# A recurrent layer in four streams: 256 places for sums and powers, two tiles of squares, and another order of the step

## The chip, the core and the metric

The kernel runs on one core of a Trainium2 chip. A core has five engines that run side by side and wait for one another through semaphores: TensorE (PE in the profile, with its weight loads shown as PEld), VectorE (DVE), ScalarE (ACT), GpSimd (POOL) and SyncE (SP), which here only starts transfers. Each engine takes its instructions strictly in the order of its own queue. The metric is the device time of the whole program in microseconds, and the figure for a kernel is the median of several runs.

## The reference, cut to what matters

The program computes four residual layers on an image of 256 x 256 places with 32 channels. The first is a gated projection behind two normalisations, the second and third are Sobel magnitudes of a pooled image behind a group norm, and the fourth, where most of the time goes, is a recurrent net of two cells over T = 256 steps and S = 256 sequences:

```python
for j in range(L):                       # L = 2 cells, hidden size H = 128
    zz = concatenate([z, h_all[j]]) @ W_cell[j] + b_cell[j]      # S x 4H
    zz = _group_norm(zz, gn_gamma[j], gn_beta[j])                # four groups of H
    i, f, o, g = split(zz, 4)
    c = sigmoid(f) * c_all[j] + sigmoid(i) * tanh(g)
    h = sigmoid(o) * tanh(c)
    z = z + h
x_hat = x_t + z @ W_out + b_out
```

So a step needs the h and the c of the step before it in each cell, and the second cell needs the h of the first.

## The kernel before, in words

The front part (loading and transposing the image, the projection layer, the two Sobel layers) takes the first 629 us of the profile. Its constants stand in one tile `kt` of 13 matrices of 128 x 128, loaded in one transfer from ACT's queue (line 99); together with the weights `wv4` and `wg4` and the small matrices `avg` and `spread` they stay in the pool `const`, which lives to the end of the program. The image `xb` is in the pool `big2`, which is closed before the recurrence (`second.close()`, line 547), so that its memory is used again.

The recurrence (function `recurrence`, from line 811) splits the work into four streams: cell l = 0 or 1, and half h = 0 or 1 of the sequences (128 each, one for each partition). I write a stream as two digits, cell and half, after the name of an operation: `sq01` is the operation `sq` of cell 0, half 1. For each stream and step there are these operations (function `one`, lines 887 to 976):

- `x` (one call, `project`, lines 866 to 885, for all four streams): bias (line 876) and input (line 879) are multiplied into a fresh PSUM bank `zz`, 128 x 512, for each stream. PE.
- `m` (line 911): the stream's own previous h times its weights is added; `i` (line 906): for cell 1, the h of cell 0 too. PE.
- `sq` (line 919): squares of `zz` are written to the stream's tile `sq`. ACT. The tiles are made once (line 760), one for each stream, with an extra column that holds epsilon for each group.
- `rd` (line 924): sums over each group give four numbers a sequence, `ve`. DVE. They go to place t % 32 of the tile `sums` (SLOTS = 32).
- `pw` (line 927): these numbers to the power -1/2, `rs`, to place t % 32 of the tile `roots`. POOL, its only work here.
- `si`, `sf`, `so`, `tg` (line 900): the gates, each 128 x 128, with `rs` as the scale. ACT. Three of them share a tile `ga`, and `so` has a tile `go`.
- `ig` (947), `fc` (951), `c` (955): the new cell state. DVE.
- `th` (line 966): tanh of the state. ACT.
- For half 0 of each cell the gate `so` and the state `c` are turned on PE first (`to`, line 959, and `T`, line 963), `th` reads the turned state, and `h` (line 969, DVE) writes the turned hidden state `hT`. For half 1, `h` is made straight (line 973, DVE), turned by `T` (line 963) and copied by `e` (line 975, DVE).
- `hs` (line 986, DVE) adds the two cells' h for the output. Every eight steps one output is made: `o0` and `o1` (lines 998 and 1008, PE), `of` (1017, ACT), `ot` (1023, DVE) and eight transfers from SP's queue.

`ga`, `go`, `fc`, `th`, `zn` and `h` come from a pool `unit` of four buffers for each name, so one for each stream. The order of everything is written out by hand: the table `PLAN` gives each operation of each stream a planned time within its step, `OUT` those of the common ones, a step is PERIOD = 7.6 later than the step before, and all of it is sorted by planned time (line 1047) and issued in that order. The planned times set the order in each engine's queue and nothing else. The two cells are therefore worked on some steps apart: in one period of 7.6 the queue holds stream 00 of step t, 01 of step t - 1 or t, and 10 and 11 of steps t - 1 to t - 3.

The code of the waits is not in the kernel text: the layer that builds the program puts a wait into each instruction that reads what another engine writes, or writes where another engine or an earlier instruction has been. An instruction carries one wait; where it needs a second one, a separate semaphore instruction stands in front of it in the same queue.

Of the kernel before, what the change touches and what calls it, by code (L numbers as in the profile page):

```python
# [11 lines left out]
F32 = mybir.dt.float32  # L12
BF16 = mybir.dt.bfloat16
AF = mybir.ActivationFunctionType
ALU = mybir.AluOpType
AX = mybir.AxisListType
PSUM = bass.MemoryType.PSUM

S = 256
T = 256  # L20
C = 32
J = 4
NB = T // J
P = 128
H = 128
L = 2
# [4 lines left out]
CELL_EPS = 1e-5  # L31


K_GN, K_CEN, K_AVG, K_SOBEL = 0, 1, 2, 3
NK = 3 + 10


# [23 lines left out]
def net_kernel(  # L61
# [33 lines left out]

    ident = cp.tile([P, P], F32, name="ident")
    make_identity(nc, ident)
    kt = cp.tile([P, NK, P], F32, name="kt")
    nc.scalar.dma_start(out=kt, in_=consts)

    def eps_tile(value, name):
        t = cp.tile([P, 1], F32, name=name)
# [17 lines left out]
    bout4 = per_channel(b_out, "bout4")  # L120

    def four_times(w, n, name):
        t = cp.tile([P, n], F32, name=name)
        for j in range(J):
            nc.gpsimd.dma_start(out=t[j * C : (j + 1) * C, :], in_=w)
        return t
# [14 lines left out]
    def busy(psum, n, rhs=None):  # L141

        junk = psum.tile([P, S], F32, name="junk", tag="junk", bufs=1)
        for _ in range(n):
            nc.tensor.matmul(
                junk, lhsT=ident, rhs=kt[:, 0:2, :] if rhs is None else rhs, start=True, stop=True
            )

    def new_stats():
# [2 lines left out]
    def group_norm(stats, psum, before, after, rhs=None):  # L152

        mv = small.tile([P, nc.vector.BN_AGGR_DIM], F32, name="mv")
        nc.vector.bn_aggr(mv, stats)
        busy(psum, before, rhs)
        pm = psum.tile([P, 1], F32, name="pm", tag="pm", bufs=1)
        nc.tensor.matmul(pm, lhsT=kt[:, K_GN, :], rhs=mv[:, 0:1], start=True, stop=True)
        busy(psum, 2, rhs)
        mean = small.tile([P, 1], F32, name="mean")  # L160
        nc.vector.tensor_copy(mean, pm)
        d = small.tile([P, 1], F32, name="d")
        nc.vector.tensor_sub(d, mv[:, 0:1], mean)
        q = small.tile([P, 1], F32, name="q")
        nc.vector.scalar_tensor_tensor(q, d, d, mv[:, 1:2], ALU.mult, ALU.add)
        pv = psum.tile([P, 1], F32, name="pv", tag="pm", bufs=1)
        nc.tensor.matmul(pv, lhsT=kt[:, K_GN, :], rhs=q, start=True, stop=True)
        busy(psum, after, rhs)
        std = small.tile([P, 1], F32, name="std")
        nc.scalar.activation(std, pv, AF.Sqrt, bias=gn_eps)  # L170
        scale = small.tile([P, 1], F32, name="scale")
        nc.vector.reciprocal(scale, std)
        bias = small.tile([P, 1], F32, name="bias")
        nc.vector.scalar_tensor_tensor(bias, mean, -1.0, scale, ALU.mult, ALU.mult)
        return scale, bias
# [1 line left out]
    KS = NST // 4  # L177


    avg = cp.tile([P, KS, KS, J], F32, name="avg")  # L180
    nc.gpsimd.memset(avg, 0.0)
    for ks in range(KS):
        nc.gpsimd.tensor_copy(avg[:, ks, ks, :], kt[:, K_AVG, 0:P:C])
    spread = cp.tile([P, KS * J, C], F32, name="spread")
    for g in range(4):
        rows = slice(g * C, (g + 1) * C)
        nc.gpsimd.tensor_copy(
# [46 lines left out]
    with tc.tile_pool(name="ln", bufs=4) as lnp:  # L234
        rstd = lnp.tile([P, 2 * S], F32, name="rstd", bufs=1)
        with tc.tile_pool(name="ps_ln", bufs=6, space=PSUM) as ps_ln, tc.tile_pool(
            name="ps_var", bufs=1, space=PSUM
        ) as ps_var:
            cen = lnp.tile([P, P], F32, name="cen", bufs=1)
            nc.vector.tensor_scalar(cen, kt[:, K_CEN, :], gn[0], None, ALU.mult)  # L240
            pcb = ps_var.tile([P, 1], F32, name="pcb")
            nc.tensor.matmul(pcb, lhsT=kt[:, K_CEN, :], rhs=gn[1], start=True, stop=True)
            cb = lnp.tile([P, 1], F32, name="cb", bufs=1)
            nc.vector.tensor_copy(cb, pcb)
            pvar = ps_var.tile([P, 2 * S], F32, name="pvar")
            sqs = {}

            def variance(k, g, ks):
                nc.tensor.matmul(
                    pvar[g * C : (g + 1) * C, :],  # L250
                    lhsT=avg[:, ks].rearrange("p k j -> p (k j)"),
                    rhs=sqs.pop(k),
                    start=ks == 0,
                    stop=ks == KS - 1,
                )

            for i, (k, g, ks) in enumerate(pairs):
                pc = ps_ln.tile([P, 2 * S], F32, name="pc")
                nc.tensor.matmul(pc, lhsT=cen, rhs=pair(xa, k), start=True, stop=True)  # L259
                sqs[k] = lnp.tile([P, 2 * S], F32, name="sq", bufs=10)  # L260
                nc.scalar.activation(sqs[k], pc, AF.Square, bias=cb)
                nc.vector.tensor_scalar(pair(xb, k), pc, cb, None, ALU.add)
                if g == 3 and ks:
                    for q in pairs[i - 7 : i - 3]:
                        variance(*q)
            for q in pairs[-4:]:
                variance(*q)
            std = lnp.tile([P, 2 * S], F32, name="std", bufs=1)
            nc.scalar.activation(std, pvar, AF.Sqrt, bias=ln_eps)
            table(AF.Sigmoid, std[:, 0:1])  # L270
            nc.vector.reciprocal(rstd, std)
            for _ in range(9):
                nc.tensor.matmul(
                    pvar[:, 0:S], lhsT=ident, rhs=kt[:, 0:2, :], start=True, stop=True
                )
        with tc.tile_pool(name="ps_sp", bufs=8, space=PSUM) as ps_sp:
            for i, (k, g, ks) in enumerate(pairs):
# [18 lines left out]
            junk = ps_sp.tile([P, 2 * S], F32, name="pb")  # L296
            for _ in range(4):
                nc.tensor.matmul(
                    junk[:, 0:S], lhsT=ident, rhs=kt[:, 0:2, :], start=True, stop=True
                )  # L300


# [441 lines left out]
class RecurrentInputs:  # L744
# [5 lines left out]
    def __init__(self, tc, ctx, xa):  # L750
        self.nc = nc = tc.nc
        self.xa = xa
        kp = ctx.enter_context(tc.tile_pool(name="keep", bufs=1, reuse_waits="tile"))
        self.mhalf = kp.tile([P, 4], F32, name="mhalf")
        nc.gpsimd.memset(self.mhalf, -0.5)

        self.sqs = {}
        for l in range(L):
            for h in range(2):
                sq = self.sqs[l, h] = kp.tile([P, 4, H + 1], F32, name=f"sq{l}{h}")  # L760
                nc.gpsimd.memset(sq[:, :, H : H + 1], CELL_EPS)
        self.xts = []
        for i in range(self.NX):
            self.xts.append(kp.tile([P, self.XT, J, P], F32, name=f"xt{i}"))
        for k in range(self.NX):
            self.load(k)
# [11 lines left out]
    def of(self, t, rows):  # L778
# [5 lines left out]


SLOTS = 32
PERIOD = 7.600
BLOCKS = 2
PLAN = {
    (0, 0): dict(  # L790
        m=0.300, sq=1.814, rd=1.883, pw=2.686, tg=4.187, sf=4.207, so=4.930, fc=5.023,
        to=5.301, si=5.390, ig=5.646, c=5.897, T=6.647, th=7.011, h=7.161,
    ),
    (0, 1): dict(
        m=4.328, sq=5.425, rd=6.234, pw=8.247, sf=8.370, tg=8.501, si=8.549, fc=8.711,
        so=8.739, ig=9.246, c=9.459, th=9.581, h=10.106, T=10.657, e=11.627,
    ),
    (1, 0): dict(
        i=10.749, m=14.225, sq=14.912, rd=15.578, pw=16.964, si=17.174, so=17.198, tg=17.865,
        to=17.992, ig=18.493, sf=18.507, fc=18.957, c=19.359, T=19.440, th=19.713, h=20.542,  # L800
    ),
    (1, 1): dict(
        i=17.550, m=17.552, sq=18.681, rd=19.727, pw=20.540, si=20.935, sf=21.284, fc=21.803,
        tg=21.870, ig=21.907, c=22.633, so=23.115, th=23.210, h=23.269, T=23.489, e=24.537,
    ),
}
OUT = dict(x=7.804, hs=31.517, o0=35.554, o1=38.043, of=39.159, ot=39.669)

def recurrence(tc, out, ident, weights, inputs, general):
# [22 lines left out]
    up = ctx.enter_context(tc.tile_pool(name="unit", bufs=4))  # L834

    kp = ctx.enter_context(tc.tile_pool(name="norm", bufs=1))
    sums = kp.tile([P, 2 * L, SLOTS, 4], F32, name="ve")
    roots = kp.tile([P, 2 * L, SLOTS, 4], F32, name="rs")
    sp = ctx.enter_context(tc.tile_pool(name="state", bufs=2))
    hp = ctx.enter_context(tc.tile_pool(name="hid", bufs=6))  # L840
    op = ctx.enter_context(tc.tile_pool(name="outp", bufs=1))
# [45 lines left out]
    def one(name, l, h, t):  # L887
# [6 lines left out]
        def gate(g, func):  # L894

            x, scale = (get("zn"), 1.0) if general else (get("zz"), get("rs")[:, g : g + 1])
            if g == 2:
                v["go", l, h] = up.tile([P, H], F32, name="go")
            dst = get("go") if g == 2 else gates(get("ga"), min(g, 2))
            nc.scalar.activation(dst, gates(x, g), func, scale=scale)  # L900
            v["left", l, h, t] -= 1
# [15 lines left out]
                )  # L917
        elif name == "sq":
            nc.scalar.activation(  # L919
                sqs[l, h][:, :, 0:H], four(get("zz")), AF.Square, scale=float(H**-0.5)  # L920
            )
        elif name == "rd":
            ve = v["ve", l, h] = sums[:, 2 * l + h, t % SLOTS, :]
            nc.vector.tensor_reduce(ve, sqs[l, h], AX.X, ALU.add)  # L924
        elif name == "pw":
            rs = v["rs", l, h] = roots[:, 2 * l + h, t % SLOTS, :]
            nc.gpsimd.tensor_tensor(rs, get("ve"), inputs.mhalf, ALU.pow)  # L927
            v["ga", l, h] = up.tile([P, 3 * H], F32, name="ga")
            if not general:
# [32 lines left out]
                v["pt", l, h] = bank("pt", ("pt", l, h), [P, 2, 2 * H])  # L962
            nc.tensor.transpose(get("pt")[:, 1, 0:P], get("c" if turned else "h"), ident)  # L963
        elif name == "th":
            th = v["th", l, h] = up.tile([P, H], F32, name="th")
            nc.scalar.activation(th, get("pt")[:, 1, 0:P] if turned else get("c"), AF.Tanh)  # L966
        elif name == "h":
            if turned:
# [124 lines left out]
```

## Time and profile before

| | |
|---|---|
| median of 3 runs | 2632.31 us (2629.91 to 2633.71) |
| the profiled execution, its own time | 2632.46 us |
| its span, first to last instruction | 2630.6 us |
| start of the first `x` of the recurrence | 628.9 us |
| start of the last `x` | 2608.3 us |
| granted TensorE clock over the span | 0.991 |
| power on POOL, line 927 | 1024 of 1023 ns |
| sum on DVE, line 924 | 1024 of 689 ns |
| squares on ACT, line 919 | 1024 of 609 ns |

In the views a row of the timeline gives the start in us, the duration in us, engine, line, operation, tiles, shapes and count, and in brackets the idle time of the engine just before it with what ended it. Durations of matmuls are modelled and overlap with the next one, so the starts tell more than the ends.

### The profile page before, as it was taken

The numbers are of one execution on the slowest core, as the hardware profiler recorded it, in microseconds if no ns is written. First come the engines' busy times: TensorE is split into PE (matmuls) and PEld (weight loads), VectorE is DVE, ScalarE is ACT, GpSimd is POOL, SyncE is SP. The second block draws the span as 40 slices with busy tenths as digits, with TensorE's granted clock in tenths as the row PEclk, the third lists the DMA queues.
The fourth block names the chain that finished last, engine by engine and source line by source line (L and its number), as shares of the span: only waits on it lengthen the run. The fifth ranks groups of instructions, "written<-read, shape, count | busy, mean of one in ns | idle before, by whom it ended". The sixth has DMA issues, their size and how long they took to land.

```text
span 2630.6 us, 43062 instructions
## 1 busy us (share of the span) xinstructions
PE 2574.9 (98%) x11181; PEld 1007.4 (38%) x11181; DVE 2329.4 (89%) x6735; ACT 2296.4 (87%) x6948; POOL 1298.0 (49%) x1288
## 2 busy tenths in 40 slices
PE   7999999998999999999999999999999999999997
PEld 4533433433333333333333333333333333333332
DVE  6788799796999999999999999999999999999996
ACT  5677677675999999999999999999999999999996
POOL 2211276463555555555555555555555555555553
PEclk9899999999999999999999999999999999999998
DMA  4000000002010000001010101010000001000000
GB/s 146 1 1 1 18 1 1 0 1 49 1 25 8 18 12 14 16 10 20 6 21 5 21 5 21 5 24 9 18 12 14 16 10 20 6 5 5 5 5 10
DMA packets 110744, 38.68 MB, mean 15 GB/s; under 512 B 74852, under 2 KB 107653, under 8 KB 110488
## 3 DMA queue, kind: packets, MB, share of 16 engines
q1 hardware_dynamic: 108452, 34.54, 6.1%
q8 instruction: 92, 1.51, 0.3%
q14 instruction: 164, 1.34, 0.2%
q10 hardware_dynamic: 1236, 0.99, 0.1%
q0 software_dynamic: 800, 0.30, 0.1%
HBM read 10.63 MB, written 8.39 MB: 7 GB/s over the span
## 4 chain that ended last, share of the span: by engine, by line
PE 93%; DVE 3%; ACT 2%; POOL 1%; issue 1%; DMA 1%; DVEq 0%; SPq 0%; ACTq 0%; POOLq 0%
PE zz L911 35%; PE zz L906 16%; PE zz L879 8%; PE pt L963 6%; PE pv L315 5%; PE pg L489 4%; PE pg L449 3%; PE zz L876 3%; PE pg L339 2%; PE pt L959 2%; PE pg L315 1%; PE px L1008 1%; PE pc L259 1%; PE px L998 1%; PE pb L280 1%
## 5 line engine op out<-in xcount | busy, mean ns | idle before, releaser
L927 POOL TENSOR_TENSOR rs<-ve,mhalf 128x4 f32<-128x4 f32 x1024 | 1047.1, 1023 | 953.5 <-DVE ve L924 953.5
L911 PE MATMUL zz<-wc,hT 128*128 128x512 f32 x2040 | 1069.0, 612 | 1.4 <-DVE hT L969 1.2
L900 ACT ACTIVATE ga<-zz,rs 128x128 f32<-128x128 f32 x3072 | 974.7, 376 | 53.6 <-POOL rs L927 47.3
L924 DVE TENSOR_REDUCE ve<-sq 128x4 f32<-128x516 f32 x1024 | 705.2, 689 | 69.4 <-ACT sq L919 49.1
L919 ACT ACTIVATE sq<-zz 128x512 f32<-128x512 f32 x1024 | 623.7, 609 | 53.8 <-PE zz L911 14.2
L906 PE MATMUL zz<-wc,hT 128*128 128x512 f32 x1024 | 524.4, 594 | 0.0
L911 PEld LDWEIGHTS zz<-wc,hT 128*128 128x128 f32 x2040 | 306.7, 189 | 355.8 <-DVE hT L969 168.7
L900 ACT ACTIVATE go<-zz,rs 128x128 f32<-128x128 f32 x1024 | 394.1, 385 | 0.0
L947 DVE TENSOR_TENSOR c<-ga 128x128 f32<-128x128 f32 x1024 | 298.4, 291 | 65.1 <-ACT ga L900 58.6
L951 DVE TENSOR_TENSOR fc<-ga,c 128x128 f32<-128x128 f32 x1020 | 297.9, 292 | 5.5 <-ACT ga L900 4.1
L955 DVE TENSOR_TENSOR c<-c,fc 128x128 f32<-128x128 f32 x1020 | 286.7, 281 | 8.8
L879 PE MATMUL zz<-fx,xt 32*128 32x512 f32 x2048 | 265.8, 589 | 0.0
L333 DVE TENSOR_TENSOR o<-pv,sg 128x512 f32<-128x512 f32 x256 | 158.1, 681 | 43.3 <-PE pg L315 37.7
L959 PEld LDWEIGHTS pt<-ident,go 128*128 128x128 f32 x512 | 71.1, 139 | 290.8 <-ACT go L900 283.4
L906 PEld LDWEIGHTS zz<-wc,hT 128*128 128x128 f32 x1024 | 172.7, 209 | 9.4 <-issue 9.4
L963 PEld LDWEIGHTS pt<-ident,c 128*128 128x128 f32 x512 | 70.9, 139 | 268.9 <-DVE c L955 260.9
L966 ACT ACTIVATE th<-c 128x128 f32<-128x128 f32 x512 | 166.0, 324 | 4.6 <-DVE c L955 1.2
L963 PE MATMUL pt<-ident,h 128*128 128x128 f32 x512 | 157.9, 308 | 10.8 <-DVE h L973 8.5
L330 ACT ACTIVATE sg<-pg 128x512 f32<-128x512 f32 x256 | 138.6, 599 | 31.0 <-PE pg L315 26.3
L966 ACT ACTIVATE th<-pt 128x128 f32<-128x128 f32 x512 | 146.2, 286 | 18.9 <-PE pt L963 18.9
L969 DVE TENSOR_TENSOR hT<-pt,th 128x128 f32<-128x128 f32 x512 | 144.1, 282 | 13.8 <-ACT th L966 13.8
L315 PE MATMUL pv<-xb,wv 32*128 32x512 f32 x512 | 156.2, 619 | 0.0
(169 smaller groups left out, 2991.6 us busy)
## 6 DMA issues: line engine op xcount, KB each, us to landing
xt<-xa SPq DMA_DIRECT2D x256, 64.0 KB, 2.0
nat<-in_x_dram SPq DMA_DIRECT2D x16, 512.0 KB, 7.1
out_dram<-st SPq DMA_DIRECT2D x252, 32.0 KB, 1.7
wc<-in_L_conv_W_cell_dram SPq DMA_DIRECT2D x2, 512.0 KB, 4.8
kt<-in_consts_dram ACTq DMA_DIRECT2D x1, 832.0 KB, 6.1
wv<-in_L_conv_Wv_dram POOLq DMA_DIRECT2D x4, 32.0 KB, 4.2
wg<-in_L_conv_Wg_dram POOLq DMA_DIRECT2D x4, 32.0 KB, 6.2
out_dram<-st ACTq DMA_DIRECT2D x4, 32.0 KB, 3.3
```

What stands on the lines that cost most here:

```text
L315: nc.tensor.matmul(ps, lhsT=w[rows, half * P : (half + 1) * P], rhs=mn, start=True, stop=True)
L879: nc.tensor.matmul(v["zz", l, h, t], lhsT=inputs.of(t, r), rhs=fx[r, :], start=False, stop=l == 0 and t == 0,)
L900: nc.scalar.activation(dst, gates(x, g), func, scale=scale)
L906: nc.tensor.matmul(get("zz"), lhsT=v["hT", 0, t][:, seqs], rhs=wc[:, l, 0, :], start=False, stop=t == 0)
L911: nc.tensor.matmul(get("zz"), lhsT=v["hT", l, t - 1][:, seqs], rhs=wc[:, l, 1, :], start=False, stop=True,)
L919: nc.scalar.activation(sqs[l, h][:, :, 0:H], four(get("zz")), AF.Square, scale=float(H**-0.5))
L924: nc.vector.tensor_reduce(ve, sqs[l, h], AX.X, ALU.add)
L927: nc.gpsimd.tensor_tensor(rs, get("ve"), inputs.mhalf, ALU.pow)
L947: nc.vector.tensor_mul(c, gates(get("ga"), 0), gates(get("ga"), 2))
L951: nc.vector.tensor_mul(fc, gates(get("ga"), 1), get("c"))
L963: nc.tensor.transpose(get("pt")[:, 1, 0:P], get("c" if turned else "h"), ident)
L966: nc.scalar.activation(th, get("pt")[:, 1, 0:P] if turned else get("c"), AF.Tanh)
```

## The change

Five things are edited together:

- `sums` and `roots` get one place for each of the 256 steps, where there were 32 (for weights of the plain case, which these inputs are).
- Each stream gets two tiles of squares, used on even and odd steps.
- `go` and `th` get eight buffers where they had four.
- `PLAN` and `OUT` are other numbers. By engine, the order within a period changes in these places. ACT: `si01` and `sf01` change places among the four gates of stream 01, `tg10` and `si10` among those of stream 10, and the order `tg00 sf00 th10 so00 si00` becomes `sf00 so00 th10 si00 tg00`; `of` comes in front of stream 01's gates instead of behind them. DVE: `ig01` stands in front of `fc01`; `hs` moves from between these two to between `h10` and `ig00`, and comes 2.9 of planned time sooner after its step; `ot` moves from in front of `e11` to in front of `h11`. PE: `o0` moves from in front of `to00` to behind it. Everything else keeps its order on each engine, POOL too.
- The first two constant matrices get a tile of their own, `kg`, with a transfer of its own in front of that of the other eleven; these eleven, `wv4`, `wg4`, `avg` and `spread` move to the pool `big2`, whose memory is free again when the recurrence begins.

```diff
-K_GN, K_CEN, K_AVG, K_SOBEL = 0, 1, 2, 3
+K_GN, K_CEN = 0, 1
+K_AVG, K_SOBEL = 0, 1
...
-    kt = cp.tile([P, NK, P], F32, name="kt")
-    nc.scalar.dma_start(out=kt, in_=consts)
+    kg = cp.tile([P, 2, P], F32, name="kg")
+    nc.scalar.dma_start(out=kg, in_=consts[:, 0:2, :])
+    kt = big2.tile([P, NK - 2, P], F32, name="kt")
+    nc.scalar.dma_start(out=kt, in_=consts[:, 2:NK, :])
...
-        t = cp.tile([P, n], F32, name=name)
+        t = big2.tile([P, n], F32, name=name)
...
-    avg = cp.tile([P, KS, KS, J], F32, name="avg")
+    avg = big2.tile([P, KS, KS, J], F32, name="avg")
...
-    spread = cp.tile([P, KS * J, C], F32, name="spread")
+    spread = big2.tile([P, KS * J, C], F32, name="spread")
...
-                sq = self.sqs[l, h] = kp.tile([P, 4, H + 1], F32, name=f"sq{l}{h}")
-                nc.gpsimd.memset(sq[:, :, H : H + 1], CELL_EPS)
+                for i in range(2):
+                    sq = self.sqs[l, h, i] = kp.tile([P, 4, H + 1], F32, name=f"sq{l}{h}{i}")
+                    nc.gpsimd.memset(sq[:, :, H : H + 1], CELL_EPS)
...
     (0, 0): dict(
-        m=0.300, sq=1.814, rd=1.883, pw=2.686, tg=4.187, sf=4.207, so=4.930, fc=5.023,
-        to=5.301, si=5.390, ig=5.646, c=5.897, T=6.647, th=7.011, h=7.161,
+        m=0.300, sq=1.315, rd=2.221, pw=2.435, sf=3.687, so=3.851, si=5.257, tg=5.350,
+        fc=5.575, to=5.625, ig=5.913, c=6.078, T=7.351, th=7.469, h=7.525,
     ),
     (0, 1): dict(
-        m=4.328, sq=5.425, rd=6.234, pw=8.247, sf=8.370, tg=8.501, si=8.549, fc=8.711,
-        so=8.739, ig=9.246, c=9.459, th=9.581, h=10.106, T=10.657, e=11.627,
+        m=5.465, sq=5.522, rd=6.135, pw=6.225, si=8.272, tg=8.393, sf=8.539, so=8.617,
+        ig=9.064, fc=9.178, c=9.275, th=9.750, h=10.406, T=11.076, e=11.164,
     ),
     (1, 0): dict(
-        i=10.749, m=14.225, sq=14.912, rd=15.578, pw=16.964, si=17.174, so=17.198, tg=17.865,
-        to=17.992, ig=18.493, sf=18.507, fc=18.957, c=19.359, T=19.440, th=19.713, h=20.542,
+        i=11.801, m=14.599, sq=15.182, rd=15.403, pw=15.916, tg=17.278, so=17.665, si=17.826,
+        sf=17.853, ig=18.025, to=18.521, fc=18.583, c=18.914, T=19.851, th=20.220, h=20.862,
     ),
     (1, 1): dict(
-        i=17.550, m=17.552, sq=18.681, rd=19.727, pw=20.540, si=20.935, sf=21.284, fc=21.803,
-        tg=21.870, ig=21.907, c=22.633, so=23.115, th=23.210, h=23.269, T=23.489, e=24.537,
+        i=17.726, m=17.895, sq=18.421, rd=19.343, pw=19.789, si=21.949, sf=21.973, fc=22.060,
+        tg=22.379, ig=22.470, c=22.779, so=22.984, th=23.047, h=23.842, T=24.141, e=24.465,
     ),
-OUT = dict(x=7.804, hs=31.517, o0=35.554, o1=38.043, of=39.159, ot=39.669)
+OUT = dict(x=7.840, hs=28.575, o0=29.152, o1=30.235, of=30.667, ot=30.900)
...
-    sums = kp.tile([P, 2 * L, SLOTS, 4], F32, name="ve")
-    roots = kp.tile([P, 2 * L, SLOTS, 4], F32, name="rs")
+    slots = SLOTS if general else T
+    sums = kp.tile([P, 2 * L, slots, 4], F32, name="ve")
+    roots = kp.tile([P, 2 * L, slots, 4], F32, name="rs")
...
-                v["go", l, h] = up.tile([P, H], F32, name="go")
+                v["go", l, h] = up.tile([P, H], F32, name="go", bufs=8)
...
-                sqs[l, h][:, :, 0:H], four(get("zz")), AF.Square, scale=float(H**-0.5)
+                sqs[l, h, t % 2][:, :, 0:H], four(get("zz")), AF.Square, scale=float(H**-0.5)
...
-            ve = v["ve", l, h] = sums[:, 2 * l + h, t % SLOTS, :]
-            nc.vector.tensor_reduce(ve, sqs[l, h], AX.X, ALU.add)
+            ve = v["ve", l, h] = sums[:, 2 * l + h, t % slots, :]
+            nc.vector.tensor_reduce(ve, sqs[l, h, t % 2], AX.X, ALU.add)
...
-            rs = v["rs", l, h] = roots[:, 2 * l + h, t % SLOTS, :]
+            rs = v["rs", l, h] = roots[:, 2 * l + h, t % slots, :]
...
-            th = v["th", l, h] = up.tile([P, H], F32, name="th")
+            th = v["th", l, h] = up.tile([P, H], F32, name="th", bufs=8)
```

The other edits only put `kg` in the place of `kt[:, 0:2, :]`, `kt[:, K_GN, :]` and `kt[:, K_CEN, :]`.

More of the change, by code (lines that the diff above doesn't have):

```diff
@@ L145, in busy @@
             nc.tensor.matmul(
-                junk, lhsT=ident, rhs=kt[:, 0:2, :] if rhs is None else rhs, start=True, stop=True
+                junk, lhsT=ident, rhs=kg if rhs is None else rhs, start=True, stop=True
             )
@@ L157, in group_norm @@
         pm = psum.tile([P, 1], F32, name="pm", tag="pm", bufs=1)
-        nc.tensor.matmul(pm, lhsT=kt[:, K_GN, :], rhs=mv[:, 0:1], start=True, stop=True)
+        nc.tensor.matmul(pm, lhsT=kg[:, K_GN, :], rhs=mv[:, 0:1], start=True, stop=True)
         busy(psum, 2, rhs)
@@ L166, in group_norm @@
         pv = psum.tile([P, 1], F32, name="pv", tag="pm", bufs=1)
-        nc.tensor.matmul(pv, lhsT=kt[:, K_GN, :], rhs=q, start=True, stop=True)
+        nc.tensor.matmul(pv, lhsT=kg[:, K_GN, :], rhs=q, start=True, stop=True)
         busy(psum, after, rhs)
@@ L239, in net_kernel @@
             cen = lnp.tile([P, P], F32, name="cen", bufs=1)
-            nc.vector.tensor_scalar(cen, kt[:, K_CEN, :], gn[0], None, ALU.mult)
+            nc.vector.tensor_scalar(cen, kg[:, K_CEN, :], gn[0], None, ALU.mult)
             pcb = ps_var.tile([P, 1], F32, name="pcb")
-            nc.tensor.matmul(pcb, lhsT=kt[:, K_CEN, :], rhs=gn[1], start=True, stop=True)
+            nc.tensor.matmul(pcb, lhsT=kg[:, K_CEN, :], rhs=gn[1], start=True, stop=True)
             cb = lnp.tile([P, 1], F32, name="cb", bufs=1)
@@ L273, in net_kernel @@
                 nc.tensor.matmul(
-                    pvar[:, 0:S], lhsT=ident, rhs=kt[:, 0:2, :], start=True, stop=True
+                    pvar[:, 0:S], lhsT=ident, rhs=kg, start=True, stop=True
                 )
@@ L298, in net_kernel @@
                 nc.tensor.matmul(
-                    junk[:, 0:S], lhsT=ident, rhs=kt[:, 0:2, :], start=True, stop=True
+                    junk[:, 0:S], lhsT=ident, rhs=kg, start=True, stop=True
                 )
@@ L786 @@
 SLOTS = 32
-PERIOD = 7.600
+PERIOD = 7.6
 BLOCKS = 2
```

## The prediction

> **What bounds the kernel now.** I read the page first, then the starts of line 876 (one group a step), then the timeline of a late and an early step, and then who waits around the tile `ve`.
>
> ```profile
> PE 2574.9 (98%) x11181; PEld 1007.4 (38%) x11181; DVE 2329.4 (89%) x6735; ACT 2296.4 (87%) x6948; POOL 1298.0 (49%) x1288
> ```
>
> PE looks full, but its ends are modelled. By starts, a late step without output lasts 7.51 us (line 876 at 1504.16 and 1511.67). PE's own work is less. From start to start in an early period (from 726.94) the seven 512-wide groups take 0.96 (line 879), 0.96 (`m00`), 0.86 (`i11`), 0.90 (`m11`), 0.87 (`i10`), 0.86 (`m01`) and 0.87 (`m10`), together 6.28; the six turns with the gaps behind them 0.77 once the wait before `T01` is left out; line 876 0.22: 7.27. The other 0.24 is waiting. What is waited for is a loop through all engines. From a late step:
>
> ```profile
> 1503.24 0.60 ACT L919 ACTIVATE sq<-zz 128x512 f32<-128x512 f32 x1
> ...
> 1503.94 0.69 DVE L924 TENSOR_REDUCE ve<-sq 128x4 f32<-128x516 f32 x1 [0.18 <-ACT sq L919]
> ...
> 1504.71 1.01 POOL L927 TENSOR_TENSOR rs<-ve,mhalf 128x4 f32<-128x4 f32 x1 [1.11 <-DVE ve L924]
> ...
> 1505.76 0.88 ACT L900 ACTIVATE ga<-zz,rs 128x128 f32<-128x128 f32 x3
> ...
> 1506.76 0.61 ACT L919 ACTIVATE sq<-zz 128x512 f32<-128x512 f32 x1
> ...
> 1507.48 0.69 DVE L924 TENSOR_REDUCE ve<-sq 128x4 f32<-128x516 f32 x1
> ...
> 1508.52 0.30 PE L963 MATMUL pt<-ident,h 128*128 128x128 f32 x1
> ...
> 1509.62 1.02 PE L911 MATMUL zz<-wc,hT 128*128 128x512 f32 x2
> ```
>
> These are `sq01`, `rd01`, `pw01`, the gates of 01, `sq00`, `rd00`, then `T01` and `m01`, whose end starts the next `sq01` at 1510.74. Start to start: `sq01` to `rd01` 0.70, to the gates 1.82 (sum, power and two hops), to `sq00` 1.00, to `rd00` 0.72, to `h01` at 1508.09 0.61, to `T01` 0.43, to `m01` 1.10 (`i10` and `T10` between), to `sq01` 1.12: together 7.50, the step. PE stands still before `T01`, and whatever shortens the loop shortens the step until PE's 7.27.
>
> Now the hop into the sum: `sq01` ends at 1503.84, `rd01` starts at 1503.94, 0.10 later. Early in the recurrence:
>
> ```profile
> 726.02 0.60 ACT L919 ACTIVATE sq<-zz 128x512 f32<-128x512 f32 x1
> ...
> 726.65 0.69 DVE L924 TENSOR_REDUCE ve<-sq 128x4 f32<-128x516 f32 x1
> ```
>
> Here it is 0.03. The view of the tile `ve` says it for all: DVE's idle time ended by the squares, first in 659 to 868 us, then in 1000 to 2500:
>
> ```profile
>   ACT sq L919: 0.4, 1
> ```
> ```profile
>   ACT sq L919: 35.1, 196
> ```
>
> The trace's semaphore instructions, 17 to 21 ns each, tell why. On DVE in front of line 924 there is none between 649 and 873.9 us, and from there four a step (777 between 1000 and 2500 us, 194 steps). That is the 32nd step, from which `rd` writes places that POOL has read and must wait for POOL as well. And the step jumps with it: 7.37 from start to start of line 876 before (726.94 to 734.31), 7.51 after; eight steps with their output 60.67 before, 61.69 after. Two hops of the loop, 0.068 each, are 0.136: all of the jump. So the kernel before holds the experiment on its first part.
>
> **What the Trainium skill says.** "Perfetto Trace Analysis", section "Identifying Dependency Chains": instructions that wait on multiple engines may have EventSemaphore instructions put in front. The trace agrees, with 15 a step in late steps: four on DVE (924), nine on ACT (900: four, 919: three, 966: two), two on PE (959 and 963). The same page, section "Per-engine timelines": a DVE or ACT instruction is pushed with its wait into a wait queue and the sequencer goes on, while a sequencer-only instruction holds its wait in the sequencer itself. So an instruction behind a semaphore that waits is only decoded once that is satisfied. The trace agrees: 0.033 us from end to start without one, 0.101 with one, and the semaphore at 1511.38 stands 0.065 ahead of its sum. "Trainium Kernel Development and Optimization", section "Performance Expectations": matmul busy time is a bad metric because matmuls are pipelined; here 98% busy goes with 0.2 us of waiting a step.
>
> **The change part by part.**
>
> *256 places.* No place is written twice, so DVE's four semaphores a step go for all steps. Two of them lie in the loop (`sq01` to `rd01`, `sq00` to `rd00`): 2 x 0.068 = 0.136 a late step; nothing in the first 32.
>
> *Two tiles of squares.* `sq` overwrites a tile that ACT wrote a step ago. For that it carries a wait on ACT itself, and the wait for PE stands in front as a semaphore (three of four a step; `sq10` needs none). With two tiles the older write is two steps back, and ACT has by then waited on itself for a later one (the first gate of each stream waits for its `ga` of a step ago). So the PE wait goes into `sq` itself. In the loop that is `m01` to `sq01`, seen as 0.061 from semaphore (1510.68) to squares (1510.74): 0.06 in every step. This hop without a semaphore is not in the trace; bounds 0 (the PE hop may not shorten) and 0.07 (as on DVE). I take 0.06.
>
> *Eight `go` and `th`.* The same for `th00` and `th11` (semaphores at line 966). `th11` starts 0.10 after `c11`; but the gates of 01 behind it wait for `pw01`, which ends 0.03 ahead of them (1505.72 and 1505.76), so 0.07 here buys nothing. `th00` feeds `h00`, which DVE's order holds. Worth 0, hidden by `pw01`; bounds 0 and 0.03.
>
> *Order.* The loop keeps its edges: all four gates of 01 still stand in front of `sq00`, `rd00` in front of `h01`, `T01 i10 T10` in front of `m01`. So swapping gates moves nothing in it. I walked through one period with the new orders, the durations above, and `rd01` at 0: gates of 01 at 1.82, `sq00` 2.82, `rd00` 3.47, `h01` 4.08, `T01` 4.51, `m01` 5.62, `sq01` 6.68, `rd01` 7.305. Beside it: `h10` 6.13, `hs` 6.33, `ig00` 6.67 (its last gate ends 6.60), `c00` 7.00, DVE free for `rd01` at 7.20, so `hs` in its new place (0.34) is covered with 0.1 to spare; uncovered it costs 0.34 a step. `T00` at 7.46, line 879 at 7.88, `m00` at 8.84, `T11` 9.79, `m11` 10.77, `to10` 11.67, so PE could give `T01` at 11.78, 0.03 ahead of the loop. `pw11` ends 0.03 late for `si11`, which has slack. The step becomes 7.305, and PE is all but full. PE's two semaphores (for `to10` and `T01`) depend on which bank is reused; the order of banks gives `T01` the same kind of owner before it, so I keep it; without it the loop is 7.25 and PE's 7.27 decides.
>
> *Output.* `o0` (0.86) and `o1` (1.00) lie on PE in one period, before and after, behind each other in front of `m00`. They cost an output step 61.69 - 8 x 7.505 = 1.65 now, because PE's slack takes up 0.2; in the early steps 1.71. With a slack of 0.04 I take 1.82. `of` now stands in front of the gates and `ot` in front of `h11`: in an output step `of` can start when `o1` ends, at 9.75, `ot` at 10.50, `h11` at 11.14, `T11` at 11.48, while the late `m00` lets PE reach `T11` only at 11.66. Covered by 0.2; without that cover up to 0.64 on 32 outputs, 20 us.
>
> *Front.* One more DMA on ACT's queue at 1.2 us (the first took 0.40 there); behind it ACT's gamma and beta loads, its table load and the first copy, which starts at 10.62 after waiting 7.32 for PE: covered. SP's and POOL's queues get nothing new there. Four more memsets on POOL at 614.2 (0.2 for four) lie far ahead of its first power at 632.2. The first input loads, SP at 613.27, may wait for the last matmul with `kt` at 613.5; the first `x` comes at 628.9, so 16 issues of 0.66 have 3 us to spare. Worth 0, at most 1.
>
> **Sum.** Late blocks of eight: 61.69 to 8 x 7.305 + 1.82 = 60.26, 1.43 less, 28 times: 40.0. Early ones: 60.67 to 60.26, four times: 1.6. Span 2630.6 - 41.7 = 2588.9, and with the 1.9 outside it the profiled execution's 2632.5 becomes 2590.8. That execution is 0.15 from the median of 2632.31, so the forecast is 2591 us.
>
> **Rivals.**
> - *Only DVE's hops count* (`sq01` stays late, or output steps grow): the early step, 7.37, throughout: 28 x 1.02 = 29 less, 2604. For: this much the trace has shown. Against: `sq01` sits 0.061 behind a semaphore.
> - *PE becomes the bound*: semaphore of `T01` gone as well, 7.27 and 1.86 an output: 28 x 1.67 + 4 x 0.65 = 49 less, 2583; if `m00`'s 0.96 holds some waiting too, down to 2574.
> - *The waits stay*: another order could need others, and the time stays at 2632. Against: nothing writes a place twice.
> - *`hs` turns into the wait* (slower): it sits in front of `ig00`, `c00`, `rd01`, and behind that `pw01`. Fully uncovered it adds its 0.34: the step is 7.645, and against 7.505 and 7.37 that is 0.14 x 224 + 0.27 x 32 = 40 more, 2672. It decides from 0.31 us of delay (its cover 0.11 and the 0.20 gained). Against: DVE idles 0.21 before `ig00` and 0.18 before `rd01`.
>
> **How the numbers follow.** Forecast (2583 to 2598) 0.55; PE as the bound (2574 to 2583) 0.15; DVE's hops alone or a part lost (2598 to 2612) 0.20; up to 2627, 0.03; waits stay 0.03; slower 0.04. A measurement can tell about 0.2%, 5 us. Faster is 0.93, same 0.03, slower 0.04. The range 2574 to 2607 leaves out about 0.15: the tail above the DVE-only case and what is below PE's bound.
>
> **What would show it.** Starts of line 876 7.30 apart; `rd` 0.03 behind `sq` in all steps; `sq01` about 0.04 behind `m01`'s end; no idle time of DVE before `rd01` ended by anything but the squares. Wrong if DVE waits before `ot` for longer than 0.5, if `rd01` starts right behind `c00`, or if steps of 7.37 stay.

## The result and the profile after

The kernel after takes **2589.2 us** (median, 2584.07 to 2592.09) against 2633.01 us (2629.91 to 2636.33) of the kernel before on the same chip: a ratio of **0.9831 [0.9809, 0.9853]**. The forecast was 2591 us in a range of 2574 to 2607.

The profiled execution of the kernel after took 2584.07 us, and its span is 2582.1 us where it was 2630.6. Its first `x` starts at 627.7 us (before 628.9), its last at 2560.1 (2608.3). So 47.0 of the 48.5 us come from the recurrence, 1.2 from the front and 0.3 from the end. The line of busy times on its page hardly shows it:

```profile
PE 2530.7 (98%) x11181; PEld 1041.5 (40%) x11181; DVE 2317.7 (90%) x6735; ACT 2282.5 (88%) x6948; POOL 1284.0 (50%) x1292
```

PE is at 98% as before, and DVE and ACT gained a point each because the span shrank. What changed is the distance between instructions. Here is the loop in the timeline of the kernel after, the same eight operations of a late step as in the prediction, with lines 4 or 5 higher (start, duration, engine, line, operation):

```profile
1499.48 0.60 ACT L924 ACTIVATE sq<-zz 128x512 f32<-128x512 f32 x1
...
1500.12 0.69 DVE L929 TENSOR_REDUCE ve<-sq 128x4 f32<-128x516 f32 x1
...
1500.88 1.01 POOL L932 TENSOR_TENSOR rs<-ve,mhalf 128x4 f32<-128x4 f32 x1 [1.04 <-DVE ve L929]
...
1501.93 0.88 ACT L905 ACTIVATE ga<-zz,rs 128x128 f32<-128x128 f32 x3
...
1502.94 0.61 ACT L924 ACTIVATE sq<-zz 128x512 f32<-128x512 f32 x1
...
1503.59 0.69 DVE L929 TENSOR_REDUCE ve<-sq 128x4 f32<-128x516 f32 x1
...
1504.62 0.30 PE L968 MATMUL pt<-ident,h 128*128 128x128 f32 x1
...
1505.73 1.02 PE L916 MATMUL zz<-wc,hT 128*128 128x512 f32 x2
```

Start to start: `sq01` to `rd01` 0.64 (before 0.70), to the gates 1.81, to `sq00` 1.01, to `rd00` 0.65 (before 0.72), over `h01` to `T01` 1.03, to `m01` 1.11, to the next `sq01` at 1506.79 1.06 (before 1.12). These are 7.31 with their rounding, and the three edges that became shorter, by 0.06 to 0.07 each, are the three that the prediction named.

The tile `ve`, between 1000 and 2500 us, had DVE's idle time ended by the squares 196 times in the kernel before. In the kernel after this view holds only POOL's own wait for the sums:

```profile
its engine sat idle before it (us, times) until:
  DVE ve L929: 697.2, 798
```

The view lists idle times above 0.15 us alone, though: DVE still stands still in front of `rd01`, for 0.03 us in the median step where it was 0.17.

The semaphore instructions in steps without an output fell from 15 to 6. On DVE none is left (4 a step before), ACT has 4 (9 before), all in front of gates of line 905, and PE has 2 as before.

### The profile page after: what moved, and what is told of

It reads as the page before. It is cut to its first block, busy times and chain, and to the rows that moved or that the text cites. A ratio compares the mean times of both kernels' runs of the same rounds, so it can differ in the third digit from the quotient of the medians.

```text
span 2582.1 us, 40860 instructions
## 1 busy us (share of the span) xinstructions
PE 2530.7 (98%) x11181; PEld 1041.5 (40%) x11181; DVE 2317.7 (90%) x6735; ACT 2282.5 (88%) x6948; POOL 1284.0 (50%) x1292
## 4 chain that ended last, share of the span: by engine, by line
PE 94%; DVE 3%; ACT 1%; DMA 1%; POOL 0%; issue 0%; DVEq 0%; SPq 0%; ACTq 0%; POOLq 0%
PE zz L916 36%; PE zz L911 17%; PE zz L884 9%; PE pt L968 5%; PE pv L318 5%; PE pg L492 4%; PE pg L452 3%; PE zz L881 3%; PE pg L342 2%; PE pt L964 2%; PE px L1013 1%; PE pg L318 1%; PE pc L262 1%; PE px L1003 1%; PE pb L283 1%; DMA nat<-in_x_dram 1%
## 5 line engine op out<-in xcount | busy, mean ns | idle before, releaser
L932 POOL TENSOR_TENSOR rs<-ve,mhalf 128x4 f32<-128x4 f32 x1024 | 1032.1, 1008 | 921.9 <-DVE ve L929 921.9
L916 PEld LDWEIGHTS zz<-wc,hT 128*128 128x128 f32 x2040 | 328.3, 190 | 398.1 <-DVE c L960 167.6
L956 DVE TENSOR_TENSOR fc<-ga,c 128x128 f32<-128x128 f32 x1020 | 292.5, 287 | 2.9 <-ACT ga L905 2.9
L911 PEld LDWEIGHTS zz<-wc,hT 128*128 128x128 f32 x1024 | 161.0, 197 | 2.8 <-issue 0.5
L980 DVE COPY hT<-pt 128x128 f32<-128x128 f32 x512 | 145.5, 284 | 8.9 <-PE pt L968 8.8
```

Of the source, the lines that this page charges most:

```text
L911: nc.tensor.matmul(get("zz"), lhsT=v["hT", 0, t][:, seqs], rhs=wc[:, l, 0, :], start=False, stop=t == 0)
L916: nc.tensor.matmul(get("zz"), lhsT=v["hT", l, t - 1][:, seqs], rhs=wc[:, l, 1, :], start=False, stop=True,)
L956: nc.vector.tensor_mul(fc, gates(get("ga"), 1), get("c"))
```

## Experiments

**How the rows are read.** "Step" is the distance between the starts of the bias matmul (line 876 before, 881 after); "early" are steps among the first 32. "Eight steps" is the median distance over eight late steps with their output. "Longer steps" are late ones without an output, of 194, that took 0.06 us or more above their median. Times with an interval of the ratio are medians; the others are single times, good to some 5 us (the four of the kernel after lie between 2584 and 2592), and there the step is the better witness. The kernels ran on several chips, on which the kernel before took 2632.66 to 2636.73 us; each ratio is taken on one chip.

| kernel | time, us | ratio to before | early step | late step | eight steps | longer steps |
|---|---|---|---|---|---|---|
| before | 2633.01 | 1 | 7.370 | 7.506 | 61.69 | 15 |
| e_front | 2630.92 | | 7.362 | 7.500 | 61.67 | 12 |
| e_order | 2632.36 | 0.9995 [0.9986, 1.0004] | 7.368 | 7.504 | 61.61 | 13 |
| e_places | 2603.26 | 0.9891 [0.9875, 0.9908] | 7.362 | 7.362 | 60.61 | 7 |
| e_squares | 2617.47 | | 7.303 | 7.439 | 61.29 | 14 |
| e_old_order | 2584.57 | 0.9815 [0.9799, 0.9831] | 7.303 | 7.302 | 60.17 | 1 |
| after | 2589.2 | 0.9831 [0.9809, 0.9853] | 7.305 | 7.305 | 60.19 | 1 |
| e_one_square | 2604.06 | | 7.369 | 7.369 | 60.66 | 3 |
| e_bufs4 | 2589.36 | | 7.310 | 7.310 | 60.23 | 8 |
| e_cell0_32 | 2614.44 | | 7.300 | 7.438 | 61.13 | 5 |
| e_cell1_32 | 2582.34 | | 7.302 | 7.301 | 60.17 | 2 |
| e_bank | 2587.69 | | 7.301 | 7.301 | 60.17 | 1 |
| e_early | 2613.72 | | 7.410 | 7.410 | 61.14 | 0 |
| e_both | 2617.48 | 0.9935 [0.9921, 0.9948] | 7.414 | 7.414 | 61.17 | 0 |

### The parts of the change, one at a time

**e_front** is the kernel before with only the constants moved.

```diff
-    kt = cp.tile([P, NK, P], F32, name="kt")
+    kg = cp.tile([P, 2, P], F32, name="kg")
+    kt = big2.tile([P, NK - 2, P], F32, name="kt")
```

> The kernel before with only the constants moved and split (32 places, one tile of squares, four buffers, old order). Loop theory (a semaphore instruction costs only where it stands in the loop of one step): nothing changes, steps of 7.37 up to the 32nd and 7.505 after it, about 2632 us. Memory theory (where the tiles lie in SBUF matters): some other step, 7.3 to 7.4, from the 33rd on.

Measured 2630.92 us beside 2632.66 of the kernel before. The first `x` started at 625.3 us, but in the other kernels it started anywhere from 626.3 to 631.3 us whichever of the two fronts they had, so neither this nor the 1.2 us of the kernel after is an effect. Moving the constants is worth nothing that shows. That the larger places need the room it makes is likely, but no run tried them without it.

**e_order** is the kernel before with only the new `PLAN` and `OUT`.

```diff
-OUT = dict(x=7.804, hs=31.517, o0=35.554, o1=38.043, of=39.159, ot=39.669)
+OUT = dict(x=7.840, hs=28.575, o0=29.152, o1=30.235, of=30.667, ot=30.900)
```

> The kernel before with only the new table of planned times. Loop theory: the loop keeps all its edges, so 7.37 and then 7.505, 2632 within 5 us. Order theory: steps near 7.3 and about 2590. If hs in its new place becomes the wait: longer steps, up to 7.64.

Measured 0.9995 [0.9986, 1.0004], with the same steps as before to 0.002 us. The order alone does nothing that shows.

**e_places** is e_front with 256 places.

```diff
-    slots = SLOTS
+    slots = SLOTS if general else T
```

> Constants moved and 256 places for sums and powers, all else as before (old order). Loop theory: DVE's four semaphore instructions a step are gone, two of them in the loop, so 7.37 in every step and 28 x 1.02 = 29 us less than before, about 2604. Order theory (the new order makes the gain): 2632.

Measured 0.9891 [0.9875, 0.9908]: the late step fell from 7.500 to 7.362 us and equals the early one, which didn't move. The jump at the 32nd step is gone, and its size of 0.138 is that of the two hops of 0.068 that the prediction read from the early steps.

**e_squares** is e_front with two tiles of squares.

```diff
-                sqs[l, h][:, :, 0:H], four(get("zz")), AF.Square, scale=float(H**-0.5)
+                sqs[l, h, t % 2][:, :, 0:H], four(get("zz")), AF.Square, scale=float(H**-0.5)
```

> Constants moved and two tiles of squares, all else as before (32 places, old order). Loop theory: the hop from m01 to sq01 is 0.06 shorter, so 7.31 up to the 32nd step and 7.445 after it, 15 us less, about 2617. If the hop from PE does not shorten without its semaphore: 7.505 and 2632.

The early step fell from 7.362 to 7.303 us and the late one from 7.500 to 7.439, 0.06 both. The jump at the 32nd step stays. So the hop from `m01` to `sq01` is worth 0.06, and the two parts add up: 0.138 + 0.06 = 0.198, and from e_front (7.500) to e_old_order below (7.302), which has both, it is 0.198.

**e_old_order** is the kernel after with the old `PLAN` and `OUT`.

> The changed kernel with the old table of planned times. Loop theory: the same loop, 7.305 to 7.32 (PE's own 7.22 to 7.27 is below that), 2589 us within 6. Order theory: the new order carries the gain, 2604 or more.

Measured 2584.57 us, 0.9815 [0.9799, 0.9831], with a step of 7.302. Its interval overlaps that of the kernel after, so the two orders aren't told apart with the waits gone either.

**e_one_square** is the kernel after with one of its two tiles of squares used, **e_bufs4** the kernel after with four buffers of `go` and `th`.

```diff
-                sqs[l, h, t % 2][:, :, 0:H], four(get("zz")), AF.Square, scale=float(H**-0.5)
+                sqs[l, h, 0][:, :, 0:H], four(get("zz")), AF.Square, scale=float(H**-0.5)
```

> The changed kernel with one tile of squares per stream again. Loop theory: the wait for PE stands in a semaphore instruction in front of sq01 again, 0.06 a step more, 7.365 and about 2604 us. If that hop costs nothing: 7.305 and 2589.

```diff
-            th = v["th", l, h] = up.tile([P, H], F32, name="th", bufs=8)
+            th = v["th", l, h] = up.tile([P, H], F32, name="th")
```

> The changed kernel with four buffers of go and th again. Two semaphore instructions a step come back on ACT, in front of th00 and th11. Loop theory: neither is in the loop (the gates behind th11 wait for the power anyway), 7.305 and 2589 us within 5. Queue theory: 0.06 or more a step, 2604 or more.

With one tile the step is 7.369, 0.064 more: the second tile is worth the same under the new order. With four buffers it is 7.310 against 7.305. But eight of its late steps are longer, where the kernel after has one, and from the first to the last `x` the trace of e_bufs4 takes 1938.0 us, that of the kernel after 1932.4. Of these 5.6 us the median step makes 1.3 and the eight longer steps 1.9. So eight buffers shorten the step by next to nothing, yet they may be worth some 5 us, which one trace of each kernel can't settle.

### Is it the number of semaphores, or where they stand?

**e_cell0_32** and **e_cell1_32** are the kernel after with 32 places again for the sums of one cell alone, which brings back two of DVE's four semaphores a step. Cell 0's stand in the loop, cell 1's do not.

```diff
-            ve = v["ve", l, h] = sums[:, 2 * l + h, t % slots, :]
+            ve = v["ve", l, h] = sums[:, 2 * l + h, t % (SLOTS if l == 0 else slots), :]
```

> The changed kernel with 32 places again for the sums of cell 0 alone (streams 00 and 01, whose sums lie in the loop); two semaphore instructions a step come back on DVE. Loop theory: both are in the loop, 7.305 up to the 32nd step and 7.44 after it, about 2619 us. Queue theory (each semaphore instruction costs its engine the same wherever it stands): the same as with cell 1, half of what all four cost, about 7.37 and 2604.

> The changed kernel with 32 places again for the sums of cell 1 alone (streams 10 and 11, whose sums are not in the loop); as many semaphore instructions come back as with cell 0. Loop theory: 7.305 in every step, 2589 us within 5. Queue theory: about 7.37 after the 32nd step and 2604.

The trace has 391 semaphore instructions in front of the sums on DVE between 1000 and 2500 us for cell 0, and 399 for cell 1. Cell 0's cost 0.138 us a step (7.300 to 7.438), cell 1's nothing (7.302 to 7.301). The single times, 2614.44 and 2582.34, lie 5 and 7 us below the expected ones. The same tile `ve`, who waited for it and how long: first in e_cell0_32, then in e_cell1_32 (engine, tile and line of the one that waited, us in all, times):

```profile
  ACT ga L905: 33.3, 171
```
```profile
  ACT ga L905: 0.2, 1
```

This looks like all or nothing, but only because the view lists idle times above 0.15 us. The gate is the first one of stream 00, behind the squares of stream 11, and it waits for the power that follows `rd00`. The ACT rows of one step, first in e_cell0_32, then in e_cell1_32:

```profile
1502.00 0.66 ACT L924 ACTIVATE sq<-zz 128x512 f32<-128x512 f32 x1
1502.85 0.37 ACT L905 ACTIVATE ga<-zz,rs 128x128 f32<-128x128 f32 x1 [0.20 <-POOL rs L932]
```
```profile
1503.64 0.63 ACT L924 ACTIVATE sq<-zz 128x512 f32<-128x512 f32 x1
1504.40 0.37 ACT L905 ACTIVATE ga<-zz,rs 128x128 f32<-128x128 f32 x1
```

In the median step ACT stands still here for 0.195 us in e_cell0_32 and for 0.128 in e_cell1_32, which is the 0.129 of the kernel after. The 0.067 between them is one hop. With cell 1's semaphores the sum of stream 10 comes later too, 1.15 us behind the start of line 881 instead of 1.09, and the step doesn't change. The number is the same, so the place decides. This is the direct test of the prediction's account. It also shows that cell 0's sums alone make the whole jump: the step is 7.438 here and 7.439 in e_squares, where all sums and powers have 32 places.

### What bounds the step now

At 7.305 the prediction put the loop just ahead of PE's own 7.27. Of PE's two semaphores one still stands in front of `T01`, so this hop should have 0.06 left to give.

**e_bank** hands out the PSUM banks for the turns so that `T01` gets one whose last reader asks for no second wait.

```diff
-            v["pt", l, h] = bank("pt", ("pt", l, h), [P, 2, 2 * H])
+            v["pt", l, h] = bank("pt", ("pt", l, h), [P, 2, 2 * H], l if len(free) > 1 else 0)
```

> The changed kernel, with to10 taking the second bank of the free list, so that T01 gets the bank that stream 11 left and to10 that of stream 01. The semaphore instruction in front of T01, which waits for h01 in the loop, is then not needed. Loop theory: 0.055 less a step, 7.25, about 2575 us. If PE alone already sets the step: 7.305 and 2589.

The semaphore went in the steps without an output, `T01` moved up, and the step stayed at 7.301. The PE rows of the timeline of e_bank from `to10` on show where the gain went:

```profile
1509.09 0.27 PE L964 MATMUL pt<-ident,go 128*128 128x128 f32 x1
1509.20 0.32 PE L968 MATMUL pt<-ident,h 128*128 128x128 f32 x1
1509.35 1.02 PE L911 MATMUL zz<-wc,hT 128*128 128x512 f32 x2
1510.22 0.33 PE L968 MATMUL pt<-ident,c 128*128 128x128 f32 x1
1510.39 1.02 PE L916 MATMUL zz<-wc,hT 128*128 128x512 f32 x2
```

`T01` starts 0.11 behind `to10`, where the kernel after has 0.19 (1504.43 and 1504.62). But the gain is given back one turn later: `m01` starts 0.17 behind `T10`, where it was 0.11 (1505.62 and 1505.73). `T10` waits for its state now. The weight loads of e_bank, with the idle time in front, and below it those of the kernel after:

```profile
1510.22 0.14 PEld L968 LDWEIGHTS pt<-ident,c 128*128 128x128 f32 x1 [0.67 <-DVE c L960]
```
```profile
1505.56 0.14 PEld L968 LDWEIGHTS pt<-ident,c 128*128 128x128 f32 x1 [0.61 <-DVE c L960]
```

In e_bank `c10` starts at 1509.88 and `m01` comes 0.51 behind it; in the kernel after `c10` starts at 1505.22, and `m01` comes 0.51 behind it, too. There the load for `T10` stood 0.06 ahead of its matmul, which waited for PE; here both start at 1510.22. So a second loop, from `sq00` over the gates of stream 10 on ACT, `c10` on DVE and `T10` to `m01`, and back to `sq01`, is as long as the first.

**e_early** attacks the first loop elsewhere: the gate `so01`, which in the loop only `h01` reads, 1.5 us later (1502.69 and 1504.19 in the kernel after), goes behind `sq00`, so that only three gates stand in front of `sq00`.

```diff
-        m=5.465, sq=5.522, rd=6.135, pw=6.225, si=8.272, tg=8.393, sf=8.539, so=8.617,
+        m=5.465, sq=5.522, rd=6.135, pw=6.225, si=8.272, tg=8.393, sf=8.539, so=8.930,
```

> The changed kernel with so01 moved behind sq00 on ACT. The loop then has three gates between the power and sq00 instead of four: 0.25 shorter, of which m00's end lets 0.13 through. Loop theory: PE's own 7.22 becomes the bound, 7.22 to 7.25, about 2571 us. If PE alone already sets the step: 7.305 and 2589. If so01 is then late for h01: no gain.

The expectation fell: the step grew to 7.410 us. `sq00` does start 1.16 behind `m00`, 0.14 sooner than the 1.30 of the kernel after. The ACT rows of the timeline of e_early, from `sq00` on, and below them those of the kernel after, from `so01` on:

```profile
1516.75 0.60 ACT L924 ACTIVATE sq<-zz 128x512 f32<-128x512 f32 x1
1517.25 0.36 ACT L905 ACTIVATE go<-zz,rs 128x128 f32<-128x128 f32 x1
1517.49 0.37 ACT L905 ACTIVATE ga<-zz,rs 128x128 f32<-128x128 f32 x1
1517.74 0.32 ACT L971 ACTIVATE th<-c 128x128 f32<-128x128 f32 x1
1517.94 0.38 ACT L905 ACTIVATE go<-zz,rs 128x128 f32<-128x128 f32 x1
1518.19 0.38 ACT L905 ACTIVATE ga<-zz,rs 128x128 f32<-128x128 f32 x1
```
```profile
1502.69 0.38 ACT L905 ACTIVATE go<-zz,rs 128x128 f32<-128x128 f32 x1
1502.94 0.61 ACT L924 ACTIVATE sq<-zz 128x512 f32<-128x512 f32 x1
1503.42 0.39 ACT L905 ACTIVATE ga<-zz,rs 128x128 f32<-128x128 f32 x1
```

The first `go` of e_early is the moved gate, 0.24 us of ACT ahead of stream 10's `tg10`. With it the last two gates of stream 10 come 2.60 behind `m00` (2.48 in the kernel after), `c10` 3.69 (3.58) and `m01` 4.19 (4.09). The 0.10 is what the step grew by. It isn't the second loop that grew, since that one passes over `so01` whether it stands in front of `sq00` or behind it. By these starts it is a third one: from `m00` over `sq00`, the gates of stream 10, `c10` and `T10` to `m01`, and on over PE's own matmuls to the next `m00` (3.22 us here, 3.21 in the kernel after). In the kernel after this loop has 0.14 to spare, in which `sq00` waits for the gates of stream 01. In e_early `sq00` waits for `m00`, whose 1.12 us end at 1516.71, and `so01` stands in the loop. No experiment has changed this loop alone.

**e_both** is e_bank and e_early together.

> Both: to10's other bank and so01 behind sq00. Loop theory: PE's own work bounds the step, 7.20 to 7.23, about 2567 us; no more than with either alone if they only reach the same bound. If the loop had nothing to do with it: 2589.

It takes 7.414 a step, 0.9935 [0.9921, 0.9948] of the kernel before: as e_early and not the 7.20 to 7.23 expected, since the third loop does not wait for `T01`. No kernel here is told apart from the kernel after on the faster side. PE's own limit, which is 7.305 less the 0.08 that it stands still before `T01`, some 7.22 as an estimate, was reached by none.

## Why the prediction was right, step by step

**The loop and its three hops: right.** The loop through all engines, not PE's 98%, set the step, and the walk of the period met the trace: 7.305 walked, 7.305 measured. 2 x 0.068 for the places stands against 0.138 in e_places, 0.06 for the squares against 0.06 in e_squares and 0.064 in e_one_square. The value 0.06 was read off a distance in one place with bounds 0 and 0.07; it held.

**The reading of the semaphores: right, with one view read too strongly.** The prediction took from the Trainium skill's "Perfetto Trace Analysis", section "Identifying Dependency Chains", that a second wait shows as an instruction of its own in front, and put a price on it from the early steps. In e_cell0_32 and e_cell1_32 the same number of them costs 0.138 a step or nothing. But the view of `ve` does not "say it for all": below 0.15 us it lists nothing, and DVE stood still in front of `rd01` for 0.105 us in the early steps and for 0.173 in the late ones. Its 1 and 196 times are a difference of 0.07; the hops of 0.03 and 0.10 carry the argument. The 17 to 21 ns of a semaphore instruction hold on ACT and in front of DVE's sums; PE's two take 51, which no sum used.

**Zero for order, front, `go` and `th`: right for the step.** e_order 0.9995, e_front without a change of the step, e_bufs4 0.005 a step, which is 1.3 us in 256 steps. Its longer steps, 1.9 us, were in no account. The slower rival, `hs` as the wait, did not come: in the kernel after `rd01` at 1507.42 follows `c00` at 1507.10 by 0.32, while back to back such a pair takes 0.20 (1505.22 to 1505.42), so 0.12 of cover is left where 0.1 was walked.

**Sizes that were off.**

- *Late blocks* fell from 61.69 to 60.19, 1.50 where 1.43 was forecast: 28 x 1.50 = 42.0 instead of 40.0. The step was right; it is the output's extra, 60.19 - 8 x 7.305 = 1.75, that was put at 1.82.
- *Early blocks* fell from 60.67 to 60.19: 4 x 0.48 = 1.9 for 1.6.
- *PE's own work* was put at 7.27. The starts in the kernel after give 7.22, with 6.22 for the seven groups instead of 6.28, so some of those of the early period had held waiting. PE has 0.08 to spare then, and not the 0.04 with which the output's extra was worked out; that this made the extra smaller is argued and not shown.
- *Left out*: the sum took each block at its median. In the kernel before, eight late steps with their output take 61.81 on average, 0.12 above the median, since 15 of 194 steps are 0.06 to 0.35 us longer; in the kernel after both are 60.19. That is 28 x 0.12 = 3.4 us that the sum did not have.

Together 47.3, where 47.0 lie between the first and the last `x`, against a forecast of 41.7. The median of the kernel after lies 5 us above its profiled execution, so the forecast's 2591 met it better than the sum deserves: part of the agreement is scatter.

**Rivals.** *Only DVE's hops count* exists as e_places: 7.362 and 2603.26 us, where 7.37 and 2604 were given; the kernel after passed it by the hop of the squares. *PE becomes the bound* did not come: the semaphore of `T01` stayed, as the prediction kept it. But the reasoning behind that rival failed: it said that without this semaphore the loop is 7.25 and PE's 7.27 decides, and e_bank gave 7.301. The walk had the second loop's parts (`c10`, `T10`) but asked only of PE and `hs` how near they were.

## What to carry to other kernels

When a kernel's engines are all nearly full, look for a loop that comes back to itself after one step and measure it start to start. Here two waits that stood in that loop cost 0.138 us a step, and two like them beside it cost nothing. A buffer that is reused soon can cost a second wait, which shows as a semaphore instruction in front of the reading or writing one: 0.06 to 0.07 us each in the loop here, and more places, or a second tile, took it away. Before shortening a loop further, list the other loops with their lengths, because the next may be tied with it, as the second was here (7.305 and 7.301), and because what leaves one loop may enter another, as in e_early. And ask of every view what it leaves out.

## What was not expected of the hardware

- Steps longer than the median go with semaphores: 15 of 194 at 15 semaphores a step, 14 at 12, 7 at 11, but 1 at 6. It isn't the number alone (8 in e_bufs4, 2 in e_cell1_32, both at 8 a step). All eight of e_bufs4 and nine of the 14 of e_squares lie multiples of 17 steps apart, so they follow some rhythm of the program; the cause is open.
- The power `pw11` took 1.083 us in the kernel before and 1.008 in the kernel after; in e_order at most 1.033; in e_early `pw00` takes 1.095. Neither lies in the first loop, and the cause is open.
- A 512-wide matmul behind a turn of 128 x 128 that had itself waited starts 0.13 to 0.17 us after it, and 0.11 after one that had not. In the kernel after `m00` starts 0.96 behind the group of line 884, and `T11` 0.96 behind `m00`, where the other 512-wide groups take 0.86.
